# Attention with two steps' values products in even steps and small work in odd ones, and with statistics and the split of q and k behind their products

## The chip, the core and the metric

The kernel runs on one core of one Trainium2 chip. The core has a matrix engine (TensorE, PE in the profile, with its weight loads as PEld), a vector engine (VectorE, DVE), a scalar engine (ScalarE, ACT), GpSimd (POOL) and SyncE (SP), which mostly issues DMA transfers. Each engine runs its own instructions in order; between engines, semaphores hold an instruction back until its inputs and its output buffer are ready. Matrix products land in PSUM, eight banks of 128 partitions x 512 fp32 values.

The metric is the device time in microseconds (us) of one execution. The kernel before takes 2402.26 us, the median of 3 runs (2398.78 to 2404.74).

## The reference

One transformer layer on `x` of shape (2, 2048, 256) in fp32, cut here to what matters:

```
qkv  = x @ qkv_w + qkv_b                 # 16 heads of 16; q and k rotated per head
attn = softmax(q @ k.T / 4) @ v          # per head, over 2048 keys
x    = layernorm(x + attn @ out_w + out_b)
n    = layernorm(x, g1, be1)
x2   = x + n + (n @ mix_w + mix_b)
n2   = layernorm(x2, g2, be2)
w    = the two largest of softmax(n2 @ router_w), others 0      # 8 experts
moe  = sum over e of w[e] * (silu(n2 @ w1[e] + b1[e]) @ w2[e] + b2[e])
out  = layernorm(x + x2 + moe)
```

Every token goes through two of eight experts. The expert stage works on lists of tokens by expert, so it can start on a list only when the tokens of the blocks before are placed.

## The kernel before

**Attention.** The work is cut into 32 visits: 2 batches x 4 blocks of 512 queries x 4 groups of 4 heads. A visit has 16 steps, one for each 128 keys, so there are 512 steps. One step does four things:

- `scores` (L466), twice, one call for each pair of heads: two products of keys and queries (L470), two that add the negative row maximum (L479), each on 64 rows of the array so that two run side by side, into the four banks of `ps_sc`; then two exponentials on ScalarE (L485) into `ex`, eight buffers.
- `maxima` (L414), twice, called the first and the second half of a step here: two products (L426) into banks of `ps_mx`, and two reduces on VectorE (L434) that take the maximum of 512 scores for each of 128 queries. These maxima are needed 20 steps later (`AHEAD`), when `scores` of the next visit starts. The three banks of `ps_mx` are handed out in turn, to the maxima and to all small work alike (`bank`, L314).
- `values` (L492): four products of `ex` and the values, one for each head, each on 32 columns of the array (L500), added up over a visit's 16 steps in one bank, `ps_av`. A product of fp32 data counts as two matmul instructions in the trace, so one call shows as eight. After step 16, `attn_out` copies the sum to `avs` on ScalarE (L515), and one step later `divide` transposes it (`ps_o`) and divides by the sums of exponentials on VectorE (L525, L526).
- small work, described below.

The order on TensorE, ScalarE, VectorE and SyncE is the order of the program. For one step it is: `scores` twice, first half of the maxima, small work, `values` of the step before, second half.

**Small work.** A small planner holds two heaps, `todo`, one for urgent items and one for others. `later(steps, fn, cost, urgent)` (L290) puts a function in, due `steps` steps from now. `work(budget)` (L295) takes due items, urgent ones first and then by due time, and takes the cost of each off the budget until it is used up; an item may exceed it. Each step calls `work(1.0)`. A group of four transposes costs 0.5, a pair of products 2.0, VectorE work alone mostly 0. The items are:

- `prep_x`, `prep_qk`, `prep_v`: transposes of `x`, the products for q and k (`ps_qk`) and the values (`ps_v`). `prep_qk` also splits its result into a high and a low part: ScalarE copies it to `full` (L352), VectorE masks the high part (L354), GpSimd subtracts (L358) and issues four DMAs to a stack in DRAM (L362). `load_k` and `load_q` read the stacks back on SyncE's queue (L388), for the visit they serve.
- `rows_of` (L455, urgent): transposes of the maxima (`ps_m`).
- a chain for each block of 512 tokens once its four groups are done, from `block` (L585): transposes (`ps_oT`), `two_products` with the output weights (`ps_p`, L561), then `norms` (L616), transposes (`ps_nT`), `two_products` with the mixing weights (`ps_mix`), `lists` (L686), transposes (`ps_n2T`), router logits (`ps_l`), the choice of two experts (`choose`, L783), places in the lists (`ps_before`), and the experts' bias (`ps_c`, `ps_b`). `two_products` (L555) adds its product to the running sum on VectorE (L568) and then takes mean and variance of two rows of 128 tokens there (`bn_stats`, `bn_aggr`, L571 and L572). `norms` and `lists` follow one step after the second product.

There are eight blocks. The chain of the last one runs in the expert stage, where `between` (L1150) moves the planner's clock on by one and calls `work(1.0)`.

**Before attention**, the weights of q and k are rotated on VectorE (L266 to L268), with the cosines and sines in `cs` and temporaries `t1` and `t2`, and the first maxima run for 20 steps alone (the lead stage, `leading[0]` true), which use the banks of `ps_sc`.

**After attention**, 46 tiles of tokens go through the experts (`hidden` L1155, `add_tile` L1172), with their weights loaded on SyncE's queue (`load_tile` L1099). The first list is made by `early_tiles` (L973), five steps after the block before the last has placed its tokens.

Of the kernel before, what the change touches and what calls it, by code (L numbers as in the profile page):

```python
# [24 lines left out]
F32 = mybir.dt.float32  # L25
# [38 lines left out]
def seq_postln_kernel(  # L64
# [88 lines left out]
    with ExitStack() as actx:  # L153
# [38 lines left out]
        with tc.tile_pool(name="wraw", bufs=1) as wp:  # L192
            wr = bp.tile([P, 2, H, 3, HD], F32, name="wr", tag="zx", bufs=1)
            cs = wp.tile([P, 2, H, 8], F32, name="cs")
# [62 lines left out]
            for c in range(2):  # L257
                for s in range(2):
                    u1, u2 = wr[:, c, :, s, 0:8], wr[:, c, :, s, 8:16]
                    for dst, a, b_, op in (  # L260
                        (wqk[:, c, s, :, 0:8], u1, u2, ALU.subtract),
                        (wqk[:, c, s, :, 8:16], u2, u1, ALU.add),
                    ):
# [74 lines left out]
        def prep_qk(b, tb, s, hh):  # L338

            full, hi = (  # L340
                ep.tile([P, 512], F32, name=k, tag=k, bufs=2) for k in ("full", "hi")
            )
            ps = bank("ps_qk", 512)
            for c in range(2):
                nc.tensor.matmul(  # L345
                    ps,
                    lhsT=wqk[:, c, s, 8 * hh : 8 * hh + 8, :].rearrange("p h d -> p (h d)"),
                    rhs=xT[b, tb][:, c, :],
                    start=(c == 0),
                    stop=(c == 1),  # L350
                )
            nc.scalar.activation(full, ps, AF.Identity, bias=bqk[:, s, hh : hh + 1])  # L352

            nc.vector.tensor_single_scalar(  # L354
                hi.bitcast(I32), full.bitcast(I32), HIGH, ALU.bitwise_and
            )
            lo = full
            nc.gpsimd.tensor_sub(lo, full, hi)  # L358
# [4 lines left out]
            stack[b, tb, s, hh] = t  # L363

# [101 lines left out]
        def scores(w, kt, pair):  # L466
# [16 lines left out]
            for j in range(2):  # L483
                ex = ap_.tile([P, 512], F32, name="ex", tag="ex", bufs=8)
# [25 lines left out]
        def attn_out(w):  # L510
# [3 lines left out]
            avs = bp.tile([P, 512], F32, name="avs", tag="avs", bufs=2)  # L514
# [40 lines left out]
        def two_products(name, turned_in, w, k, sum_, mv):  # L555
# [29 lines left out]
        def block(b, qb):  # L585
# [30 lines left out]
        def norms(n, xr, mv, eng, pitch, gap):  # L616
# [447 lines left out]
        with tc.manual_schedule(engines={ET.PE, ET.Activation, ET.DVE, ET.SP}):  # L1064
# [6 lines left out]
            before = None  # L1071
            for t in range(NSTEP):
# [258 lines left out]
```

## Time and profile before

The profiled execution took 2406.82 us; its span, from first to last instruction, is 2405.1 us. All rows are of that execution.

| what | value |
|---|---|
| profiled execution, its span | 2406.82 us, 2405.1 us |
| lead stage ends, first step starts | 123.69 us |
| last step starts | 1793.27 us |
| last group of the expert stage's products (L1176) starts | 2360.48 us |
| VectorE reduces of the maxima (L434) | 2048 x 682 ns |
| ScalarE exponentials (L485) | 2048 x 603 ns |
| VectorE `bn_stats` (L571), `bn_aggr` (L572) | 64 x 411 ns, 64 x 182 ns |
| VectorE add of a product (L568) | 32 x 688 ns |
| VectorE mask (L354), GpSimd subtraction (L358) | 32 x 440 ns, 32 x 1279 ns |

A mean of one instruction includes its start and end latency, so instructions of one kind that follow each other start closer together than their duration. A matmul's end is modelled in the profile: it is safer to read the distance between the starts of successive groups than a duration. From first to last step 1670 us go by, 69% of the span; the granted clock of TensorE is 0.76 in the stretch 60 to 120 us, 0.90 in 120 to 180, and 1.00 in nearly all later stretches of attention.

### The profile page before, as it was taken

How to read it: one execution, taken by the hardware profiler on the slowest of the kernel's cores; microseconds unless marked ns; L12 is line 12 of the kernel's file. 1: busy time of each engine (PE TensorE's matmuls, PEld its weight loads, DVE VectorE, ACT ScalarE, POOL GpSimd, SP SyncE). 2: the span in 40 equal slices, each digit the busy share in tenths (PEclk: the TensorE clock that was granted, in tenths of full speed). 3: DMA queues.
4: the chain of work that ended last, by engine and by line, in shares of the span. 5: the costliest groups of instructions: out<-in, count | busy, mean ns of one | idle time of the engine just before them, and what ended most of it. 6: DMA issues, size and time to landing. Idle time of an engine off the chain costs nothing.

```text
span 2405.1 us, 39739 instructions
## 1 busy us (share of the span) xinstructions
PE 2277.9 (95%) x14270; PEld 1363.8 (57%) x14270; DVE 1534.9 (64%) x3060; ACT 1374.4 (57%) x2722; POOL 512.7 (21%) x863
## 2 busy tenths in 40 slices
PE   5899999999999999999999999999998899999993
PEld 2444555545545555555555555555547788888883
DVE  2678778868877887888888888888825111111113
ACT  1167667757766776777777667777773222223333
POOL 6212221140123022011211202202122322222113
PEclk7799999999999999999999999999999899999997
DMA  7516541141124211111311211221045466567994
GB/s 217 153 42 182 144 115 54 54 132 53 53 72 123 87 55 58 58 45 54 115 45 54 71 45 53 89 71 53 1 138 168 142 193 180 176 182 225 291 292 151
DMA packets 175516, 269.69 MB, mean 112 GB/s; under 512 B 29776, under 2 KB 109656, under 8 KB 175320
## 3 DMA queue, kind: packets, MB, share of 16 engines
q1 hardware_dynamic: 142648, 213.26, 25.9%
q0 software_dynamic: 32256, 52.98, 10.1%
q8 instruction: 113, 1.85, 0.3%
q10 hardware_dynamic: 416, 0.92, 0.1%
q14 instruction: 83, 0.68, 0.1%
HBM read 204.29 MB, written 62.74 MB: 111 GB/s over the span
## 4 chain that ended last, share of the span: by engine, by line
PE 77%; DVE 16%; DMA 3%; ACT 2%; issue 1%; POOL 1%; another core or an unknown queue 0%; SPq 0%; ACTq 0%; DVEq 0%; POOLq 0%
PE av L500 19%; PE ps_mx L426 13%; DVE pm L434 12%; PE ps_h L1161 11%; PE ps_y L1176 10%; PE ps_sc L470 6%; PE ps_sc L479 6%; PE ps_qk L345 2%; DMA st<-full 2%; PE ps_v L371 1%; PE ps_p L561 1%; PE ps_mix L561 1%; PE ps_m L458 1%; PE ps_o L522 1%; PE ps_b L766 1%
## 5 line engine op out<-in xcount | busy, mean ns | idle before, releaser
L434 DVE TENSOR_REDUCE pm<-ps_mx 128x1 f32<-128x512 f32 x2048 | 1273.2, 682 | 218.3 <-PE ps_mx L426 209.3
L485 ACT ACTIVATE ex<-ps_sc 128x512 f32<-128x512 f32 x2048 | 1058.1, 603 | 453.7 <-PE ps_sc L479 433.7
L426 PE MATMUL ps_mx<-km,qm 64*128 64x512 f32 x2048 | 580.5, 474 | 36.4 <-DMA km<-st 15.3
L426 PEld LDWEIGHTS ps_mx<-km,qm 64*128 64x128 f32 x2048 | 297.7, 186 | 556.2 <-DVE pm L434 357.4
L500 PE MATMUL av<-ex,vt 128*32 128x512 f32 x4096 | 547.3, 606 | 0.0
L470 PE MATMUL ps_sc<-qm,km 64*128 64x512 f32 x2048 | 435.4, 396 | 0.4 <-ACT ex L485 0.3
L479 PE MATMUL ps_sc<-mrow,sel 64*128 64x512 f32 x2048 | 428.6, 392 | 0.0
L1168 ACT ACTIVATE hT<-ps_h,b 128x256 f32<-128x256 f32 (+1 forms) x368 | 156.3, 425 | 378.3 <-PE ps_h L1161 361.9
L1161 PE MATMUL ps_h<-xT,w 128*128 128x256 f32 (+1 forms) x1472 | 282.6, 342 | 17.2 <-issue 11.0
L1161 PEld LDWEIGHTS ps_h<-xT,w 128*128 128x128 f32 x1472 | 231.6, 193 | 62.4 <-ACT hT L1168 21.7
L1176 PE MATMUL ps_y<-w,hT 128*128 128x256 f32 x1136 | 253.7, 379 | 0.0
L479 PEld LDWEIGHTS ps_sc<-mrow,sel 64*128 64x128 f32 x2048 | 216.7, 185 | 40.5
L470 PEld LDWEIGHTS ps_sc<-qm,km 64*128 64x128 f32 x2048 | 214.8, 186 | 42.0 <-ACT ex L485 18.3
L1176 PEld LDWEIGHTS ps_y<-w,hT 128*128 128x128 f32 x1136 | 212.1, 190 | 27.5 <-issue 0.7
L1140 DVE TENSOR_SCALAR xT<-ps_x,cols_sb 128x256 f32<-128x256 f32 (+1 forms) x92 | 40.2, 478 | 271.4 <-PE ps_x L1136 271.4
L1187 POOL DMA_INDIRECT acc<-y,xg x71 | 110.1, 1551 | 390.8 <-DVE y L1186 307.0
L500 PEld LDWEIGHTS av<-ex,vt 128*32 128x32 f32 x4096 | 80.9, 108 | 133.7 <-issue 132.6
L1186 DVE TENSOR_SCALAR y<-ps_y,xg 128x256 f32<-128x256 f32 x71 | 34.2, 483 | 187.8 <-PE ps_y L1176 187.6
L132 POOL TENSOR_SCALAR op_mul<-mv 128x4 f32<-128x4 f32 x18 | 4.2, 233 | 492.7 <-DVE mv L572 491.7
L358 POOL TENSOR_TENSOR full<-full,hi 128x512 f32<-128x512 f32 x32 | 40.9, 1279 | 239.5 <-DVE hi L354 239.4
L345 PE MATMUL ps_qk<-xT,wqk 128*128 128x512 f32 x128 | 73.3, 700 | 4.8 <-ACT xT L336 1.5
L857 POOL DMA_INDIRECT x_list<-zx,at_i x64 | 64.1, 1002 | 16.5 <-issue 13.6
(198 smaller groups left out, 1160.4 us busy)
## 6 DMA issues: line engine op xcount, KB each, us to landing
w<-in_w SPq DMA_DIRECT2D x92, 1024.0 KB
km<-st SPq DMA_DIRECT2D x256, 256.0 KB
st<-hi POOLq DMA_DIRECT2D x64, 256.0 KB
st<-full POOLq DMA_DIRECT2D x64, 256.0 KB
qm<-st SPq DMA_DIRECT2D x64, 256.0 KB
xg<-x_list SPq DMA_DIRECT2D x25, 258.0 KB
x_in<-in_x SPq DMA_DIRECT2D x8, 512.0 KB
xr<-in_x SPq DMA_DIRECT2D x8, 512.0 KB
```

The lines of the kernel that those rows point to most:

```text
L345: nc.tensor.matmul(ps, lhsT=wqk[:, c, s, 8 * hh : 8 * hh + 8, :].rearrange("p h d -> p (h d)"), rhs=xT[b, tb][:, c, :], start=(c == 0), st ...
L426: nc.tensor.matmul(ps[j], lhsT=qm[w][pair][r, qt * P : (qt + 1) * P], rhs=km[w][pair][r, kb * 512 : (kb + 1) * 512], start=True, stop=True,)
L434: nc.vector.tensor_reduce(pm[w][:, qt, 2 * pair + j, kb : kb + 1], ps[j], AX.X, ALU.max)
L470: nc.tensor.matmul(sc[j], lhsT=km[w][pair][r, kt * P : (kt + 1) * P], rhs=qm[w][pair][r, :], start=True, stop=False,)
L479: nc.tensor.matmul(sc[j], lhsT=sel[pair][r, :], rhs=mrow[w][r, :], start=False, stop=True)
L485: nc.scalar.activation(ex, sc[j], AF.Exp, scale=0.25)
L500: nc.tensor.matmul(av[32 * h : 32 * h + 32, :], lhsT=vt[b][:, kt, at : at + 32], rhs=exs[h], start=(kt == 0), stop=(kt == 15),)
L857: ins = nc.gpsimd.indirect_dma_start(out=x_list, out_offset=bass.IndirectOffsetOnAxis(ap=at_i[:, k, i : i + 1], axis=0), in_=zx[:, k, i, : ...
L1161: nc.tensor.matmul(ps, lhsT=w1t[:, c, k * P : (k + 1) * P], rhs=xT[:, c, :], start=(c == 0), stop=(c == 1),)
L1168: nc.scalar.activation(hT[:, k, :], ps, AF.Silu, bias=b1[:, k : k + 1])
L1176: nc.tensor.matmul(ps, lhsT=hT[:, k, s * P : (s + 1) * P], rhs=w2t[:, k, :], start=(k == 0), stop=(k == NFC - 1),)
L1187: nc.gpsimd.indirect_dma_start(out=acc, out_offset=bass.IndirectOffsetOnAxis(ap=xg[:, s, D : D + 1].bitcast(I32), axis=0), in_=y, in_offse ...
```

## The change

The main loop, the planner's `work` and four places in the small work change.

1. **Main loop.** Exponentials of a step go to a list, `waiting`. In an even step no small work with a cost runs; items of cost 0 that are due are run (`work(0)`), and then `values` for all waiting steps. In an odd step `work(1.0)` runs; if it spent less than 0.4, items of cost 0 and the waiting values follow as in an even step, else the values wait for the next step, which then has two of them. `ex` gets twelve buffers in place of eight.
2. **`work`** returns what it spent, and with a budget of 0 takes items of cost 0 alone.
3. **`prep_qk`**: after the lead stage, the mask, the subtraction and the four DMAs to the stack are an item of their own, one step later.
4. **`two_products`**: the statistics of its two rows of tokens become two items, one and two steps later; `norms` and `lists` come three steps after the second product in place of one.
5. **Buffers**: `avs` has one in place of two; `cs` and the temporaries of the rotation (now `rot`, with four pairs) share the memory of `x2` and `fT`, which the chain uses later.

```diff
-            cs = wp.tile([P, 2, H, 8], F32, name="cs")
+            cs = bp.tile([P, 2, H, 8], F32, name="cs", tag="x2", bufs=1)
+            rot = bp.tile([P, 4, 2, H, 8], F32, name="rot", tag="fT", bufs=1)
...
-                        t1 = wp.tile([P, H, 8], F32, name="t1", tag="t1", bufs=2)
-                        t2 = wp.tile([P, H, 8], F32, name="t2", tag="t2", bufs=2)
+                        t1, t2 = rot[:, 2 * (s % 2) + k, 0], rot[:, 2 * (s % 2) + k, 1]
...
         def work(budget):
+
+            spent = 0.0
             for heap in todo:
-                while heap and heap[0][0] <= now[0] and budget > 0:
-                    _, _, cost, fn = heappop(heap)
-                    fn()
-                    budget -= cost
+                kept = []
+                while heap and heap[0][0] <= now[0] and (spent < budget or budget == 0):
+                    item = heappop(heap)
+                    if budget == 0 and item[2] > 0:
+                        kept.append(item)
+                        continue
+                    item[3]()
+                    spent += item[2]
+                for item in kept:
+                    heappush(heap, item)
+            return spent
...
-            for r, part in enumerate((hi, lo, hi, lo) if s == 0 else (hi, hi, lo, lo)):
-                nc.gpsimd.dma_start(out=t[:, r], in_=part)
             stack[b, tb, s, hh] = t
+
+            def split():
+
+                nc.vector.tensor_single_scalar(
+                    hi.bitcast(I32), full.bitcast(I32), HIGH, ALU.bitwise_and
+                )
+                lo = full
+                nc.gpsimd.tensor_sub(lo, full, hi)
+                for r, part in enumerate((hi, lo, hi, lo) if s == 0 else (hi, hi, lo, lo)):
+                    nc.gpsimd.dma_start(out=t[:, r], in_=part)
+
+            if leading[0]:
+                split()
+            else:
+                later(1, split)
...
-                ex = ap_.tile([P, 512], F32, name="ex", tag="ex", bufs=8)
+                ex = ap_.tile([P, 512], F32, name="ex", tag="ex", bufs=12)
...
-            avs = bp.tile([P, 512], F32, name="avs", tag="avs", bufs=2)
+            avs = bp.tile([P, 512], F32, name="avs", tag="avs", bufs=1)
...
-            for i in range(2 * k, 2 * k + 2):
+
+            def moments(i):
                 st = bp.tile([P, 6], F32, name="st", tag="st", bufs=3)
                 nc.vector.bn_stats(st, sum_[:, i, :])
                 nc.vector.bn_aggr(mv[:, i, :], st)
+
+            for i in range(2):
+                later(1 + i, lambda i=i: moments(2 * k + i))
...
-                    later(1, lambda: norms(n, xr, mv, eng, pitch, gap))
+                    later(3, lambda: norms(n, xr, mv, eng, pitch, gap))
...
-                    later(1, lambda: lists(n, xr, x2, mv2, eng, gap))
+                    later(3, lambda: lists(n, xr, x2, mv2, eng, gap))
...
-            before = None
+
+            waiting: list = []
             for t in range(NSTEP):
                 now[0] = t
                 w, kt = divmod(t, 16)
                 exs = scores(w, kt, 0) + scores(w, kt, 1)
                 max_step(t + AHEAD, 0)
-                work(1.0)
-                if before is not None:
-                    values(*before)
+                if t % 2 == 0 or work(1.0) < 0.4:
+                    work(0)
+                    while waiting:
+                        values(*waiting.pop(0))
                 max_step(t + AHEAD, 1)
-                before = (w, kt, exs)
-            values(*before)
+                waiting.append((w, kt, exs))
+            while waiting:
+                values(*waiting.pop(0))
```

More of the change, by code (lines that the diff above doesn't have):

```diff
@@ L259, in seq_postln_kernel @@
                     u1, u2 = wr[:, c, :, s, 0:8], wr[:, c, :, s, 8:16]
-                    for dst, a, b_, op in (
-                        (wqk[:, c, s, :, 0:8], u1, u2, ALU.subtract),
-                        (wqk[:, c, s, :, 8:16], u2, u1, ALU.add),
-                    ):
-                        t1 = wp.tile([P, H, 8], F32, name="t1", tag="t1", bufs=2)
-                        t2 = wp.tile([P, H, 8], F32, name="t2", tag="t2", bufs=2)
+                    for k, (dst, a, b_, op) in enumerate(
+                        (
+                            (wqk[:, c, s, :, 0:8], u1, u2, ALU.subtract),
+                            (wqk[:, c, s, :, 8:16], u2, u1, ALU.add),
+                        )
+                    ):
+                        t1, t2 = rot[:, 2 * (s % 2) + k, 0], rot[:, 2 * (s % 2) + k, 1]
                         nc.vector.tensor_mul(t1, a, cs[:, 0])
@@ L352, in prep_qk @@
             nc.scalar.activation(full, ps, AF.Identity, bias=bqk[:, s, hh : hh + 1])
[L354 to L358, printed above, removed]
             name = f"st_{b}_{tb}_{s}_{hh}"
             t = dp.tile([8, 4, HD, 512], F32, name=name, tag=name)
-            for r, part in enumerate((hi, lo, hi, lo) if s == 0 else (hi, hi, lo, lo)):
-                nc.gpsimd.dma_start(out=t[:, r], in_=part)
             stack[b, tb, s, hh] = t
+            def split():
+                nc.vector.tensor_single_scalar(
+                    hi.bitcast(I32), full.bitcast(I32), HIGH, ALU.bitwise_and
+                )
+                lo = full
[6 more added lines that the diff above has]
+                later(1, split)
         def prep_v(b, kt):
```

## The prediction

> **What bounds the kernel now.** I read the busy shares first, then busy time by stretch, then the timeline of a few steps. The page's shares say TensorE:
>
> ```profile
> PE 2277.9 (95%) x14270; PEld 1363.8 (57%) x14270; DVE 1534.9 (64%) x3060; ACT 1374.4 (57%) x2722; POOL 512.7 (21%) x863
> PE 77%; DVE 16%; DMA 3%; ACT 2%; issue 1%; POOL 1%; another core or an unknown queue 0%; SPq 0%; ACTq 0%; DVEq 0%; POOLq 0%
> ```
>
> The second line is the chain that ended last: VectorE is 16% of it, nearly all L434. The stretch 1020 to 1080 us (columns: length, then busy us of each engine, granted clock, DMA) shows why it isn't idle behind TensorE:
>
> ```profile
> 1020.00:1080.00 60.00, 58.80 (x412) 30.74 (x404) 51.77 (x96) 43.08 (x85) 10.47 (x20) 1.00 0.13 45
> ```
>
> VectorE is busy 86% where the whole page says 64%. The timeline of one plain step (start, duration, engine, line) shows how the two interlock:
>
> ```profile
> 1042.37 0.52 PE L426 MATMUL ps_mx<-km,qm 64*128 64x512 f32 x2
> ...
> 1042.81 1.06 PE L500 MATMUL av<-ex,vt 128*32 128x512 f32 x8
> ...
> 1043.81 0.50 PE L426 MATMUL ps_mx<-km,qm 64*128 64x512 f32 x2
> ...
> 1044.15 0.39 PE L470 MATMUL ps_sc<-qm,km 64*128 64x512 f32 x2
> ...
> 1044.35 2.48 DVE L434 TENSOR_REDUCE pm<-ps_mx 128x1 f32<-128x512 f32 x4 [0.22 <-PE ps_mx L426]
> ```
>
> From first half to values 0.44 us, values to second half 1.00, to the scores 0.34, and the scores take 0.92 (next first half at 1045.07): 2.70. Four reduces take 2.48, so VectorE has 0.22 to spare. A reduce starts 0.53 after its product (1043.81 to 1044.35), the next follows 0.60 later, and one lasts 0.68. Of the 512 steps 309 are plain; transposes add 0.77 (3.46), `ps_o` 0.83 (3.52), a 512-wide product pair (`ps_p`, `ps_mix`, `ps_qk`, `ps_v`) 2.1 (4.80).
>
> **What a double values product costs.** The end of attention has two values products in a row:
>
> ```profile
> 1794.75 0.16 PEld L500 LDWEIGHTS av<-ex,vt 128*32 128x32 f32 x8 [0.36 <-issue]
> 1794.75 2.51 PE L500 MATMUL av<-ex,vt 128*32 128x512 f32 x16
> 1795.21 0.13 PEld L500 LDWEIGHTS av<-ex,vt 128*32 128x32 f32 x2 [0.30 <-ACT ex L485]
> ```
>
> The second one's first weights go in 0.46 after the start, while the first still streams (1.06); one pass is some 0.43, so a second product adds 2 x 0.43 = 0.85, not 1.00. Here a rule speaks against the change: the Trainium skill ("TensorE: Matmul & The Clock Gate", section "The mechanism") lets weights load beside a running matmul only when row groups differ, and these four column tiles share all rows. By it the second product costs 1.00 again; by the row 0.85. With 153 double products that is 23 us. I take the row. The same skill ("TensorEngine Tiling (Array Packing)", "Key Properties") says that a change of tiling mode drains the array. That drain is what a double product saves, and the rows price it at only 0.15 (1.00 less 0.85) on one side and about 0.10 on the other (0.33, where nothing is late, less the 0.23 between row-tiled pairs). If small work leaves the array as values do, which I assume since eight 256-wide products take 1.93 to `av` (L561) and also 1.93 to L426 in the lead stage (104.96 to 106.89), a merged pair saves 0.15: 153 x 0.15 = 23 us at best.
>
> **What it uncovers.** Only odd steps with small work drop their values; in the changed order 153 of 256 pairs do, the others keep one product per step. In such an odd step nothing long stands between first and second half. Both halves and the small work rotate through three banks of `ps_mx`: first half takes banks 1 and 2, small work 3, second half 1 and 2 again. So the second half waits for the reduces of the first. Before, the 1.00 of the values covered that. The trace has one step without values, the first:
>
> ```profile
> 126.37 1.05 PE L426 MATMUL ps_mx<-km,qm 64*128 64x512 f32 x3
> ...
> 127.06 2.48 DVE L434 TENSOR_REDUCE pm<-ps_mx 128x1 f32<-128x512 f32 x4 [1.64 <-PE ps_sc L479]
> 127.81 0.79 PE L426 MATMUL ps_mx<-km,qm 64*128 64x512 f32 x1 [0.39 <-DVE pm L434]
> ```
>
> There the fourth product waits for the first reduce: 127.06 + 0.68 is 127.74, released 0.07 later. With small work holding the third bank it would wait for the second reduce.
>
> Let T be the start of the first half in an odd step. Reduces run T+0.53 and T+1.13 to T+1.81; the last product of the second half starts at T+1.86. Transposes alone would have let it start at T+0.62+0.58+0.11 = T+1.31. After such a late product the scores run split; the row shows the price:
>
> ```profile
> 1002.12 0.18 PEld L426 LDWEIGHTS ps_mx<-km,qm 64*128 64x128 f32 x1 [0.17 <-ACT oT L548]
> ...
> 1003.16 0.61 PE L426 MATMUL ps_mx<-km,qm 64*128 64x512 f32 x2
> ...
> 1003.70 1.06 PE L500 MATMUL av<-ex,vt 128*32 128x512 f32 x8
> ```
>
> 1.57 from the late product to the values. A pair (T to the next T) is then 1.86 + 1.57 + 1.85 + 1.26 = 6.54 (1.85 = 1.00 + 0.85; 1.26 = 0.34 + 0.92). Before, a plain step and one with transposes were 2.69 + 3.46 = 6.15. **The pair loses 0.39.**
>
> By kind, in the same way:
> - Two transposes groups, which now fall into one odd step (2 x 0.5 of budget): the last product needs the first group's bank, and ScalarE empties it only after four exponentials, which end at T+1.86, plus 0.71 to 0.80. 7.3 to 7.4, before 2 x 3.46 = 6.92.
> - Product pairs: the second half is ready at T+0.62+1.93 = 2.55, past any reduce. The add (0.69) delays the reduces behind it, and the even step's first half waits 0.3. 7.55 against 4.80 + 2.70 = 7.50, without the statistics.
> - VectorE work d between the halves of an odd step makes the even step wait d - 0.63: `rd`, `otok` (0.67) nothing worth counting; with a pair of statistics (0.59) 0.63; with the second choice (1.4) 1.47.
> - In a plain step d costs the next one d - 0.21: statistics 0.38, first choice (five small ops, 1.05) 0.84.
>
> **Moved work.** The statistics, 0.59 per row block, leave the step of their product. Before, they made the following steps 3.10, 3.19, 4.34 (with `ps_m` and the norms behind it), 3.16 and 3.07 for 2.70, 2.70, 3.46, 2.70, 2.70: 2.6 us in 64 steps, which I credit wholly; the smaller waits where they land are debited above. The split of q and k (0.44 on VectorE, 1.28 on GpSimd, four GpSimd DMA issues of 0.6) comes one step later, about 3 us: loads of `km` and `qm` are due many steps behind, and TensorE waits for `km` once, 15.3 us in all, in the lead stage, where the split stays in place. SyncE only receives later dependencies. Cost nothing; if a load were late, one wait of up to 3 us. VectorE's wait for `full` (77.4 us in all) isn't on the path: the product after it is later still. The start's buffers (`cs`, `rot`) leave the 24 rotation ops of 0.28 as they are: -1 to +1, I take 0. Twelve `ex` buffers only permit the delay. One `avs` buffer: its transposes come a step after the copy and the next copy 15 later: 0.
>
> **The sum.** I take the 64 steps 256 to 319, one whole chain of small work; the trace has them in 1193.51 - 988.98 = 204.5 us. After: four pairs with `ps_o` 6.6, 6.6, 7.2, 8.0; three with double transposes 22.1; four product pairs 30.2; three with `ps_m` 19.8; `ps_m` with the logits 7.8; `ps_c` 6.5; two with `ps_b` 13.2; the step with `ps_before` 3.5; 27 plain steps 72.6 and their waits 2.0. Sum 206.2: 1.7 more. Seven chains lie in attention: +12. The remainder: eight `ps_o`/`ps_m` pairs before the first chain +3; some 27 pairs with `ps_qk` or `ps_v`, -0.2 each, -6; four double `x` transposes +2. The expert stage keeps its 1.73 per eight products. Its first lists come five steps (12 us) later: loads issued at 1771.7 had about 26 us to the stage's start, a first weight of 1 MB at that stretch's 178 GB/s needs 6, so 0 to +5: +2. Total +13. The profiled execution took 2406.8 (span 2405.1), so it would be about 2420; from the median of the runs, 2402.3, **2415**.
>
> **Rivals.** 0.3%, 7 us, is what a measurement of this kernel can tell from no change.
> - Forecast, slower by 3 to 26 us: 53%, of which 5 lie under 7 us.
> - **The bank wait hardly forms (faster).** Place: second half of the odd step. Without any bank waits the 64 steps would take some 10.5 us less (0.64 for each short pair, 0.85 for each double transpose, and the 2.2 of waits behind `ps_o`). If half is hidden, -5.2 + 1.7 = -3.5, times 7, is -25 and with the remainder 2376. It decides once the last product starts before about T+1.77, since 13 us over 153 pairs is 0.09 each. For it: double products leave VectorE idle in even steps. Against: three banks do not let it work ahead into odd ones. 20%.
> - The second values product pays 1.00, by the rule: +23, so 2438. Against it is one instance with the row above, which ran without maxima. 15%.
> - Gains in the chain's statistics and losses of banks cancel, within 7 us: 12%.
>
> That little merges is no separate case: 153 is counted from the order. So faster 20%, same 17%, slower 63%. The range 2385 to 2440 leaves out half of the bank rival and the worst of the third.
>
> **What would show it.** After: 16-matmul groups of values with 1.85 to the next product; in odd steps L426 idle behind L434 some 0.5 us, and odd steps of 2.9 us where 2.5 would do; double transposes with L426 waiting for ScalarE. If odd steps last 2.5, the bank step is wrong and the time goes under 2395; if the double product takes 2.0, the third case holds. Steps after `ps_p` should be free of backlog; if 3.1 remains there, the credit of 2.6 is wrong.

## The result, and the profile after

The changed kernel takes **2415.75 us** (median of 7 runs, 2411.35 to 2420.32), the kernel before 2402.26 in the same series (7 runs, 2397.18 to 2410.99). The ratio is **1.0047, 95% interval 1.0031 to 1.0062**: slower by some 11 us by the ratio (13.5 between the medians). The forecast was 2415. In a later series both came out lower, 2398.07 and 2387.03, with the same ratio, 1.0047 (1.0033 to 1.0062). Its chip is called the second here; on which chip the first series ran is not on record. The level is not the chip's alone: in a third series, on the second chip, the kernel before took 2406.58 (one run).

The page of the changed kernel, first the busy shares, then the chain that ended last:

```profile
PE 2262.1 (94%) x14270; PEld 1373.1 (57%) x14270; DVE 1535.3 (64%) x3060; ACT 1376.2 (57%) x2722; POOL 512.3 (21%) x863
PE 78%; DVE 10%; ACT 5%; DMA 3%; issue 1%; POOL 1%; another core or an unknown queue 0%; SPq 0%; ACTq 0%; POOLq 0%; DVEq 0%
```

The busy times hardly move: the work is the same. TensorE's busy time fell by 15.8 us while the span grew by 4.5, so by the page the new time is TensorE waiting. In the chain VectorE fell from 16% to 10% (12% and 8% are the reduces of the maxima, L434 and L452) and ScalarE rose from 2% to 5%. The prediction had let ScalarE hold back TensorE only where two groups of transposes fall into one step.

Lines have moved: L444 is the product of the maxima (L426 before), L452 their reduce (L434), L488 and L497 the scores, L503 the exponentials (L485), L518 the values (L500), L476 and L478 the turning of the maxima and its copy to `mrow`.

A step is counted here from the first product of its scores to that of the next step. The distance from the first step's first product to the last step's, and what lies behind it, in three pairs of profiled executions (us; the expert column is from the first to the last turned tile):

| run | first step starts | 512 steps | expert stage | span |
|---|---|---|---|---|
| before | 123.7 | 1669.6 | 554.4 | 2405.1 |
| after | 120.2 | 1691.0 | 541.4 | 2409.6 |
| before, second chip | 122.5 | 1668.6 | 537.4 | 2384.7 |
| after, second chip | 121.8 | 1683.0 | 534.2 | 2396.4 |

Attention lost 21.4 and 14.4 us; 11 were forecast (12 for seven chains, less 1). The expert stage gave 3.2 us back on the second chip, where 2 were forecast as a loss. The 13.0 of the first pair are mostly not the change's: in both its profiles, in the stretch 1850 to 1900 us, ScalarE stood idle ahead of its activation of `hT` for a releaser that the profile only calls "remote" (10.4 us in two waits before, 14.1 in three after), and TensorE was busy 39.31 of 50 us at a granted clock of 0.83 before, 42.30 at 0.93 after. It fell on both kernels, and by 10 us unequally: the expert stages are 17.0 and 7.2 longer than on the second chip. The two kernels with short reduces (the last experiment) show it too, though they ran on the second chip:

```profile
ACT hT L1168 <- remote: 10.4, 2, 5.2
ACT hT L1168 <- remote: 10.6, 3, 5.8
```

The first line is of the kernel before, the second of the kernel before with short reduces (waited for: us in total, times, longest); their expert stages last 554.4 and 554.3. So the wait is not bound to a chip. The other ten profiles do not have it. The four that do are also those in which no time of landing of a DMA is recorded, so the releaser may be a DMA; that stays open.

Of the 511 steps that can be compared in the two profiles of the changed kernel, 487 repeat to 0.02 us, but 14 single ones differ by 0.4 to 1.6 and hold 7.8 of the 8.0 us between 1691.0 and 1683.0. So the reading below rests on steps, and on medians of runs for totals; an attention that differs by a few us in single profiles shows nothing by itself.

### The profile page after: what moved, and what is told of

Its sections match the earlier page's. It is cut to its first block, busy times and chain, and to the rows that moved or that the text cites. A ratio compares the mean times of both kernels' runs of the same rounds, so it can differ in the third digit from the quotient of the medians.

```text
span 2409.6 us, 39733 instructions
## 1 busy us (share of the span) xinstructions
PE 2262.1 (94%) x14270; PEld 1373.1 (57%) x14270; DVE 1535.3 (64%) x3060; ACT 1376.2 (57%) x2722; POOL 512.3 (21%) x863
## 3 DMA queue, kind: packets, MB, share of 16 engines
q8 instruction: 113, 1.85, 0.3%
## 4 chain that ended last, share of the span: by engine, by line
PE 78%; DVE 10%; ACT 5%; DMA 3%; issue 1%; POOL 1%; another core or an unknown queue 0%; SPq 0%; ACTq 0%; POOLq 0%; DVEq 0%
PE av L518 19%; PE ps_mx L444 15%; PE ps_h L1186 10%; PE ps_y L1201 10%; DVE pm L452 8%; PE ps_sc L488 8%; PE ps_sc L497 7%; ACT ex L503 3%; PE ps_qk L356 2%; DMA st<-full 2%; PE ps_v L389 1%; PE ps_p L579 1%; PE ps_mix L579 1%; PE ps_b L788 1%; PE ps_x L1161 1%
## 5 line engine op out<-in xcount | busy, mean ns | idle before, releaser
L452 DVE TENSOR_REDUCE pm<-ps_mx 128x1 f32<-128x512 f32 x2048 | 1278.2, 682 | 278.2 <-PE ps_mx L444 268.5
L503 ACT ACTIVATE ex<-ps_sc 128x512 f32<-128x512 f32 x2048 | 1057.9, 602 | 467.9 <-PE ps_sc L497 446.9
L444 PE MATMUL ps_mx<-km,qm 64*128 64x512 f32 x2048 | 600.9, 473 | 65.5 <-DMA km<-st 16.5
L444 PEld LDWEIGHTS ps_mx<-km,qm 64*128 64x128 f32 x2048 | 302.7, 186 | 517.8 <-DVE pm L452 318.5
L518 PE MATMUL av<-ex,vt 128*32 128x512 f32 x4096 | 516.3, 603 | 0.0
L488 PE MATMUL ps_sc<-qm,km 64*128 64x512 f32 x2048 | 449.0, 400 | 0.1
L497 PE MATMUL ps_sc<-mrow,sel 64*128 64x512 f32 x2048 | 439.4, 394 | 0.0
L1186 PE MATMUL ps_h<-xT,w 128*128 128x256 f32 (+1 forms) x1472 | 276.2, 337 | 11.1 <-ACT hT L1193 6.4
L497 PEld LDWEIGHTS ps_sc<-mrow,sel 64*128 64x128 f32 x2048 | 228.2, 186 | 41.8
L488 PEld LDWEIGHTS ps_sc<-qm,km 64*128 64x128 f32 x2048 | 223.0, 186 | 37.6 <-ACT ex L503 15.6
L518 PEld LDWEIGHTS av<-ex,vt 128*32 128x32 f32 x4096 | 96.8, 109 | 188.1 <-issue 186.3
```

Of the source, the lines that this page charges most:

```text
L444: nc.tensor.matmul(ps[j], lhsT=qm[w][pair][r, qt * P : (qt + 1) * P], rhs=km[w][pair][r, kb * 512 : (kb + 1) * 512], start=True, stop=True,)
L452: nc.vector.tensor_reduce(pm[w][:, qt, 2 * pair + j, kb : kb + 1], ps[j], AX.X, ALU.max)
L488: nc.tensor.matmul(sc[j], lhsT=km[w][pair][r, kt * P : (kt + 1) * P], rhs=qm[w][pair][r, :], start=True, stop=False,)
L497: nc.tensor.matmul(sc[j], lhsT=sel[pair][r, :], rhs=mrow[w][r, :], start=False, stop=True)
L503: nc.scalar.activation(ex, sc[j], AF.Exp, scale=0.25)
L518: nc.tensor.matmul(av[32 * h : 32 * h + 32, :], lhsT=vt[b][:, kt, at : at + 32], rhs=exs[h], start=(kt == 0), stop=(kt == 15),)
```

## What the steps show

**The double values product costs what the row of the prediction said.** Timeline of the changed kernel at the end of a double step (start, duration, engine, line):

```profile
997.86 1.92 PE L518 MATMUL av<-ex,vt 128*32 128x512 f32 x16
...
999.71 0.49 PE L444 MATMUL ps_mx<-km,qm 64*128 64x512 f32 x2
```

1.85 from the values to the next first half, so 0.85 for the second product. An even step whose odd neighbour uncovered nothing lasts 3.55, which is 2.70 + 0.85. And a pair with `ps_qk` takes 3.80 + 3.56 = 7.36, 0.14 under the 7.50 of before: that is the 0.15 of the merged pair.

**The bank wait on VectorE forms as forecast.** The same visit, an odd step with `ps_o`, whose first half starts at 994.41:

```profile
994.41 0.51 PE L444 MATMUL ps_mx<-km,qm 64*128 64x512 f32 x2
...
995.67 0.18 PEld L444 LDWEIGHTS ps_mx<-km,qm 64*128 64x128 f32 x1 [0.17 <-DVE pm L452]
...
996.21 0.18 PEld L444 LDWEIGHTS ps_mx<-km,qm 64*128 64x128 f32 x1 [0.36 <-DVE pm L452]
996.22 0.29 PEld L488 LDWEIGHTS ps_sc<-qm,km 64*128 64x128 f32 x2
```

Each weight load of the second half stands behind one reduce. The last is released 1.80 after the first half's start; forecast was T + 1.86. From first half to first half the odd step takes 2.83, where 2.9 was forecast (2.74 from scores to scores).

**In a step with `ps_m` another engine holds the bank.** An odd step whose first half starts at 1034.35:

```profile
1034.13 2.06 ACT L503 ACTIVATE ex<-ps_sc 128x512 f32<-128x512 f32 x4 [1.66 <-PE ps_sc L497]
1034.35 0.57 PE L444 MATMUL ps_mx<-km,qm 64*128 64x512 f32 x2
...
1035.61 0.49 PE L444 MATMUL ps_mx<-km,qm 64*128 64x512 f32 x1
1036.06 0.62 ACT L478 CAST mrow<-ps_m 128x512 fp32r<-128x512 f32 x1
...
1036.73 0.49 PE L444 MATMUL ps_mx<-km,qm 64*128 64x512 f32 x1 [0.62 <-ACT mrow L478]
```

`ps_m` was done at about 1035.7 (1035.02 + 0.66), but its copy is queued on ScalarE behind four exponentials and starts at 1036.06. The last product of the second half waits for that copy, not for a reduce, and starts 2.38 after T. The step takes 3.3 to 3.4. With two groups of transposes the same occurs, as forecast:

```profile
1002.69 1.29 ACT L566 ACTIVATE oT<-ps_oT,rows_sb 128x512 f32<-128x512 f32 x2
1003.45 0.50 PE L444 MATMUL ps_mx<-km,qm 64*128 64x512 f32 x2 [0.62 <-ACT oT L566]
```

Its first half starts at 1000.97, so the second half comes 2.48 later.

By kind, for the most frequent kinds, one pair being an odd step and the even one behind it (us; means on the second chip; the last column is the run long_only, told below):

| small work | pairs | forecast | after | long_only |
|---|---|---|---|---|
| `ps_o` | 22 | 6.6 to 8.0 | 6.92 | 6.34 |
| `ps_m` | 17 | 6.54 | 7.14 | 6.36 |
| `ps_c` | 4 | 6.54 | 7.02 | 6.23 |
| `ps_b` | 11 | 6.54 | 6.69 | 6.66 |
| two of `ps_oT`, `ps_nT` | 14 | 7.3 to 7.4 | 7.30, 7.27 | 6.75, 6.79 |
| `ps_p`, `ps_mix` | 26 | 7.55 | 7.54, 7.57 | 7.54, 7.57 |
| `ps_qk`, `ps_v` | 21 | 7.30 | 7.36, 7.36 | 7.36, 7.36 |

Where ScalarE empties one group (`ps_m`, `ps_c`) the forecast was 0.5 to 0.6 short; elsewhere it stood within 0.15.

## The experiments

The theory under test had three parts: values moved away from the odd step uncover bank waits of VectorE and ScalarE (a loss); the second values product costs 0.85; delayed statistics are a gain, as the prediction had credited them. The rivals gave the loss to one engine alone, or held that the statistics gain nothing by themselves.

### Statistics alone, values alone, and values only behind long work

Statistics alone: the kernel before with part 4 of the change.

```diff
-            for i in range(2 * k, 2 * k + 2):
+            def moments(i):
...
+            for i in range(2):
+                later(1 + i, lambda i=i: moments(2 * k + i))
...
-                    later(1, lambda: norms(n, xr, mv, eng, pitch, gap))
+                    later(3, lambda: norms(n, xr, mv, eng, pitch, gap))
...
-                    later(1, lambda: lists(n, xr, x2, mv2, eng, gap))
+                    later(3, lambda: lists(n, xr, x2, mv2, eng, gap))
```

> The kernel before with the delay of the statistics alone (two items one and two steps later, norms and lists three steps after their second product). Theory A: the delay frees VectorE's queue behind each product pair (2.6 us per chain of 64 steps, seven chains in attention: -18) and gives the last chain room in the expert stage (-13 in the trace of the changed kernel): 2402 - 31 = about 2371, within 2365 to 2385. Rival B: the statistics land in plain steps that have only 0.2 us of VectorE to spare, so attention gains under 5 us, and the expert stage's gain comes from the odd-step planning and not from the delay: 2395 to 2405.

Values alone: the changed kernel with the diff above reversed, and the split in place.

```diff
-            if leading[0]:
-                split()
-            else:
-                later(1, split)
+            split()
```

> The changed kernel with statistics, norms, lists and the split of q and k back at their product's step: only the double values products, the odd-step planning and the buffers remain. Theory A: attention loses the bank waits (+21 measured) and also the 18 us that the delay had given back, and the expert stage its -13: 2402 + 21 + 18 = about 2440, within 2430 to 2450. Rival B (the delay brings nothing): as the changed kernel or some us below, 2405 to 2418.

Values only behind long work: the changed kernel, in which transposes, `ps_o`, `ps_m` and the like keep the values beside them, and only a step that spent 1.9 or more drops them.

```diff
-                if t % 2 == 0 or work(1.0) < 0.4:
+                if t % 2 == 0 or work(1.0) < 1.9:
```

> The changed kernel with the limit for dropping the values raised from 0.4 to 1.9, so that only odd steps with a product pair drop them; transposes, logits and bias keep their values beside them. Theory A: short odd steps no longer uncover a wait for a bank of ps_mx, product pairs never had one (7.54 measured against 7.50 before); the delay's gains stay: 2415 - 21 - 18 = about 2376, within 2365 to 2388. Rival C (the loss lies in the halved number of steps open to small work, not in banks): stays at 2410 to 2420.

Measured on one chip, before at 2385.28:

| run | time | ratio (95%) | 512 steps | expert stage |
|---|---|---|---|---|
| stats_only | 2377.76 | 0.9969 (0.9958 to 0.9981) | 1666.1 | 534.6 |
| values_only | 2437.24 | 1.0223 (1.0206 to 1.0240) | 1719.5 | 537.4 |
| long_only | 2359.03 | **0.9893 (0.9875 to 0.9911)** | 1645.4 | 532.6 |

By the ratio theory A had 0.987, 1.016 and 0.989. It missed for the statistics (31 us expected, 7 found; rival B, at 2395 to 2405, stands at its edge), was right in direction and short in size for the values (52 us lost, 28 to 48 expected), and was met by long_only, where rival C falls.

Two parts of a change don't add up here. In the old order the statistics' delay brings attention nothing that can be told from the spread: 1666.1 against 1668.6, but 1665.4 in last_chain_only (below), which leaves attention as it was. The steps show why. The step behind the first `ps_p` of a chain and the two after it (steps 262 to 264) take 3.12 + 2.70 + 2.70 = 8.52 in before on the second chip, and 2.70 + 2.91 + 2.92 = 8.53 in stats_only. A plain step of stats_only in which a row block's statistics land (lines as in the kernel):

```profile
1005.55 0.41 DVE L572 BATCH_NORM_STATS2 st<-xr 128x6 f32<-128x256 f32 x1
...
1006.10 2.45 DVE L434 TENSOR_REDUCE pm<-ps_mx 128x1 f32<-128x512 f32 x4
...
1006.81 0.18 PEld L426 LDWEIGHTS ps_mx<-km,qm 64*128 64x128 f32 x1 [0.28 <-DVE pm L434]
```

An old plain step has 0.22 of VectorE to spare, so statistics that leave one step make the next product of maxima late in another. Moving the values without the two delays costs 51 us (1719.5 to 1668.6). So the delay of the statistics is worth nothing in the old order, and much in the new one (22.7 us, below).

long_only beats both kernels. Its 58 double steps lie only behind work that covers the reduces (3.80 in the odd step). Two groups of transposes keep the values between the halves, and ScalarE empties the first group's bank meanwhile:

```profile
981.15 0.50 PE L444 MATMUL ps_mx<-km,qm 64*128 64x512 f32 x2
...
982.87 1.29 ACT L566 ACTIVATE oT<-ps_oT,rows_sb 128x512 f32<-128x512 f32 x2
982.95 1.06 PE L518 MATMUL av<-ex,vt 128*32 128x512 f32 x8
...
983.94 0.50 PE L444 MATMUL ps_mx<-km,qm 64*128 64x512 f32 x2
```

The second half starts 0.99 after the values, without a wait. The pair takes 4.05 + 2.70 = 6.75 in place of 7.30 in the changed kernel and 2 x 3.46 = 6.92 before. Against the changed kernel the table above accounts for the gain: (6.92 - 6.34) x 22 + (7.14 - 6.36) x 17 + some 0.5 x 22 for the double transposes + 0.8 x 4 for `ps_c` is 40; the two attentions differ by 37.6. Against the kernel before, attention gained 23.2 us, of which the 0.14 of a merged pair, 58 times, is 8. How the rest is shared by the delays was not tested: long_only was not run without them.

### The last chain alone

The statistics of only the last block come later, in the kernel before. It is to tell what the expert stage has of it.

```diff
+                if len(ends) == NTB:
+                    later(1 + i, lambda i=i: moments(2 * k + i))
+                else:
+                    moments(2 * k + i)
...
-                    later(1, lambda: lists(n, xr, x2, mv2, eng, gap))
+                    later(3 if n == NTB - 1 else 1, lambda: lists(n, xr, x2, mv2, eng, gap))
```

> The kernel before with the delay of statistics, norms and lists for the last block alone, which runs beside the experts. Theory A: the expert stage's gain of 13 us is this delay, which lets TensorE meet the last chain's transposes after their inputs are ready: about 2389, attention unchanged (last step starts at 1793 again). Rival B: the gain came from other changes in that stretch; within 4 us of 2402.

It gave 2380.59, 0.9975 (0.9964 to 0.9985), with 1665.4 for attention and 532.6 for the expert stage: some 6 us less than before, between theory A (13) and rival B (at most 4).

The delay of the last chain does shorten the expert stage, by 3 to 5 us. The seven profiles that have it, without a remote wait and with the copy of `ps_c` on ScalarE (see below), take 532.6 to 534.6 us; the two without it, before on the second chip and values_only, both take 537.4. In these two TensorE stands idle for 3.9 us ahead of the second tile's products (L1161 in before), in the seven for 1.0.

The prediction's +2 us was for something else, the first lists, which this run leaves where they were. They are late in the changed kernel: there the first expert's weights are asked for 8.0 us before the last step starts, in before 19.6 (both on the second chip). Yet the first turned tile comes 4.66 us after that start in both. Late lists cost nothing.

### The pair again on a second chip, and the split's delay

The kernels before and after were run unchanged beside the next two, to hold profiles from one chip against each other.

> The kernel before, for a profile on the chip of this comparison. Attention should last 1669 us from first to last step again, as its steps repeat to 0.01 us; what differs from the first profile (554 us between the first and last turned tile of the experts) is the chip's or the execution's. If the changed kernel's gain of 13 us in the expert stage was real, this stage is longer here than in the changed kernel on the same chip by some 13 us; if it was the two executions', by under 6.

> The changed kernel, for a profile on the same chip: attention 1691 us again. Total against before: 1.0047 if the first comparison holds (+11 us); +16 to +20 if the expert stage's gain was only 5 us, as the delay of the last chain alone brought it.

The kernel before against itself gave 1.0003 (0.9994 to 1.0012), the changed one 1.0047 (1.0033 to 1.0062). The profiles are in the table of the first section. The expert stages differ by 3.2, so the 13 us of the first pair were mostly the two executions'. Attention came to 1683.0 for the 1691 expected, by the 14 single steps told there.

The split's delay: the changed kernel with `split()` in place, the statistics still delayed.

```diff
-            if leading[0]:
-                split()
-            else:
-                later(1, split)
+            split()
```

> The changed kernel with the mask, subtraction and DMAs of q and k back at their product's step. Theory D: without values in the step, VectorE's mask waits for ScalarE's copy of the product, which comes after four exponentials, and the second half's reduces wait behind the mask; the 64-step stretches 0 to 192 get back to 228, 225 and 225 us from 220, 219 and 220, so +18 us on the changed kernel, and stretches from 192 on stay as they are. Rival: these 18 us are the statistics' (inline in values_only too), then under +4.

2409.49, 1.0103 (1.0085 to 1.0121), attention 1696.8 against 1683.0: the delay is worth **13.8 us** (11.4 between the medians of the runs), where the prediction counted nothing. It lies in the first 192 steps, where `ps_qk` is: 21 even steps behind a `ps_qk` take 4.19 to 4.24 in place of 3.56, 14.0 us in all. Theory D had 18, as it laid the whole loss of these steps in values_only to the split; 5.9 of it is the statistics'. Its timeline in no_split_delay, lines counted as in that kernel:

```profile
316.22 0.50 PE L441 MATMUL ps_mx<-km,qm 64*128 64x512 f32 x2
...
316.38 0.69 ACT L363 ACTIVATE full<-ps_qk,bqk 128x512 f32<-128x512 f32 x1 [0.83 <-issue]
...
317.10 0.43 DVE L370 TENSOR_SCALAR hi<-full 128x512 int32<-128x512 int32 x1 [1.65 <-ACT full L363]
...
317.44 2.48 DVE L449 TENSOR_REDUCE pm<-ps_mx 128x1 f32<-128x512 f32 x4
...
318.18 0.50 PE L441 MATMUL ps_mx<-km,qm 64*128 64x512 f32 x1 [0.32 <-DVE pm L449]
318.61 1.92 PE L515 MATMUL av<-ex,vt 128*32 128x512 f32 x16
```

VectorE stands idle 1.65 us at the mask, because ScalarE writes `full` only at 316.38 to 317.07. ScalarE had been idle for 0.83 us before that, so the copy waits for the product, and not for exponentials as theory D had it. The reduces of the odd step's second half (its products start at 316.22) queue behind the mask, start at 317.44 in place of about 316.75, and the first half of the even step waits for their banks: its second product starts at 318.18. The wait for `full` was known in the kernel before, and set aside with "the product after it is later still". That held there. A step that drops its values brings the next product forward, and what was idle time at no cost becomes part of the path.

In this order the parts of the change in attention are: values moved +50.9, statistics delayed -22.7 (1719.5 to 1696.8), split delayed -13.8, together +14.4. They add up because each is the difference of two neighbours; in another order the shares would differ, as stats_only shows. values_only ran on another chip than the rest.

### The copies of ScalarE

Two copies that empty small work on ScalarE go to VectorE in the changed kernel.

```diff
-                nc.scalar.copy(t, ps)
+                nc.vector.tensor_copy(t, ps)
...
-                nc.scalar.copy(cT, ps)
+                nc.vector.tensor_copy(cT, ps)
```

> The changed kernel with the copies of ps_m and ps_c moved from ScalarE to VectorE. Theory E: in odd steps with ps_m or ps_c the last product of the second half waits for the bank of the small work, which ScalarE empties only after its four exponentials; on VectorE the copy follows the first half's reduces, so these odd steps fall from 3.3 to 3.4 to about 2.8, and some 25 pairs gain 0.3 to 0.5 each: 8 to 12 us less than the changed kernel. Rival (the wait is VectorE's own reduces): no gain, or a loss of some 0.1 a pair for 0.6 us more on VectorE.

Odd steps with `ps_m` fell from 3.38 to 2.89 and those with `ps_c` from 3.26 to 2.74, as a bank wait behind ScalarE would have it. Attention took 1677.5, 5.5 less, which is within what two executions of the changed kernel differ by. But the time was 2407.64, 1.0087 (1.0070 to 1.0104), 9.6 more than the changed kernel where theory E had 8 to 12 less: the expert stage took 548.8 in place of 534.2. The waits of TensorE from 1800 to 1920 us (waited for: us in total, times, longest), and the row of 1860 to 1880 (columns as in the prediction's such row):

```profile
PE ps_b L788 <- DVE cT L780: 10.0, 1, 10.0
```

```profile
1860.00:1880.00 20.00, 9.96 (x26) 6.48 (x25) 12.00 (x61) 1.23 (x3) 15.12 (x17) 0.66 0.28 100
```

TensorE idles half of these 20 us, at a granted clock of 0.66, because the last block's copy of `ps_c` stands on VectorE behind the making of lists. An engine that empties a bank sooner in attention empties another one later, 60 us after the last step.

### The copy of the maxima alone

To part the two effects, only the first of the two edits, in the changed kernel and in long_only:

> The changed kernel with the copy of ps_m to mrow alone on VectorE; the copy of ps_c stays on ScalarE. Theory (in odd steps with ps_m the last product of the second half waits for ScalarE's copy, behind four exponentials; what vector_copies lost in the expert stage came from the copy of ps_c in the last block): odd steps with ps_m near 2.9 us in place of 3.4, attention 1677 to 1681 us, experts 532 to 538, ratio to before 1.002 to 1.004. Rival (the 0.4 to 0.5 us come back one step later, as VectorE's reduces stand behind the copy): odd steps near 2.9 but attention 1683 +- 1, ratio 1.0047. Second rival (the loss in the expert stage came from any copy moved to VectorE): experts near 549, ratio near 1.009.

> The kernel in which only product pairs drop their values (long_only, ratio 0.9893), with the copy of ps_m to mrow on VectorE. Theory: steps with ps_m keep their values here, whose 1.00 us already covers the copy, so nothing is to be gained: ratio 0.988 to 0.991, steps with ps_m 3.6 to 3.7. Rival (ScalarE is late for the exponentials in these steps, so relieving it helps): ratio below 0.987.

maxima_copy_only: 2395.76, 1.0037 (1.0023 to 1.0050), attention 1682.2, expert stage 532.6. The expert stage's loss was the copy of `ps_c`, then. In attention the first rival is right in part: odd steps with `ps_m` take 2.89 in place of 3.38, but the even ones behind them 3.96 in place of 3.77, so 0.19 of the 0.49 comes back. The timeline of one such step:

```profile
1082.33 1.09 PE L444 MATMUL ps_mx<-km,qm 64*128 64x512 f32 x2
1082.78 0.68 DVE L478 CAST mrow<-ps_m 128x512 fp32r<-128x512 f32 x1
...
1083.38 2.48 DVE L452 TENSOR_REDUCE pm<-ps_mx 128x1 f32<-128x512 f32 x4
...
1084.12 0.18 PEld L444 LDWEIGHTS ps_mx<-km,qm 64*128 64x128 f32 x1 [0.20 <-DVE pm L452]
```

The second half no longer waits for ScalarE, but the reduces stand behind the copy, and the next step's products wait for them. A pair is 6.85 in place of 7.14; over 17 pairs 5 us, of which the whole attention shows 0.8: pairs with `ps_o` (+0.08 each) and a few single slow steps have the rest. The interval overlaps that of the changed kernel, so the total is unresolved. The wait behind ScalarE is shown; that the other engine could save it in the total is not.

long_maxima_copy: 2359.55, 0.9881 (0.9866 to 0.9896), attention 1647.7 against long_only's 1645.4. There values still lie between `ps_m` and the second half, and steps with `ps_m` take 3.65 in both. Nothing was to be gained, and nothing was.

### Reduces of a quarter of the length

In the kernels before and after the reduce of the maxima reads 128 of 512 keys, so three quarters of the keys are left out of the maxima. This makes VectorE fast and leaves TensorE's and ScalarE's work as it is.

```diff
-                    pm[w][:, qt, 2 * pair + j, kb : kb + 1], ps[j], AX.X, ALU.max
+                    pm[w][:, qt, 2 * pair + j, kb : kb + 1], ps[j][:, 0:128], AX.X, ALU.max
```

> The kernel before with each reduce of the maxima over 128 of its 512 scores, so that VectorE's part of a step falls from 2.5 to some 1.2 us; the maxima then cover a quarter of the keys. Both theories: plain steps lose the 0.1 us in which the last product of the first half waits for a reduce, 2.70 to 2.59, and the steps with waits behind VectorE's small work (3.1 to 3.5) fall to that too; attention about 1669 - 0.11 x 490 - 40 = 1575.

> The changed kernel with the same narrow reduces. Theory A: odd steps with ps_o, which waited for a reduce, fall from 2.74 to about 2.5; odd steps with ps_m, ps_c and two transposes wait for ScalarE's copy after four exponentials and stay within 0.1 of 3.4, 3.26, 3.5 to 3.75; so the changed kernel still takes more in attention than the kernel before with the same reduces, by 5 to 25 us. Rival F (reduces alone cause the loss): all short odd steps fall to about 2.5, and attention lies 20 us or more below that of the kernel before with the same reduces.

One run each gave 2251.41 and 2270.83, with attention at 1528.8 and 1562.9. If VectorE's banks were all that the changed order loses to, it should have come level or ahead with short reduces. It is 34 us behind in attention, more than with long ones and than the 5 to 25 expected. Both expectations were missed in size: attention of before fell by 140 us where 94 were expected, as steps with small work fell by more (3.46 to 3.17) than plain ones (2.70 to 2.58). And in narrow after the odd step with `ps_m` fell to 2.17 like that with `ps_o`, where the wait for ScalarE's copy was expected to keep it at 3.4. That wait had moved, into the even step:

```profile
959.58 0.62 ACT L478 CAST mrow<-ps_m 128x512 fp32r<-128x512 f32 x1
...
959.77 0.18 PEld L488 LDWEIGHTS ps_sc<-qm,km 64*128 64x128 f32 x1 [0.23 <-ACT ex L503]
...
960.25 0.19 PEld L444 LDWEIGHTS ps_mx<-km,qm 64*128 64x128 f32 x2 [0.19 <-ACT mrow L478]
```

The scores now wait for a bank that an exponential empties, and the first half for `mrow`. The pair takes 2.17 + 3.74 = 5.91 against 2.58 + 3.17 = 5.75 in narrow before. An odd step of 2.17 leaves ScalarE hardly more than the 2.07 of its four exponentials, and a copy of 0.62 on top does not fit. More than half of the 34 us comes from the 22 pairs with two groups of transposes. There the wait stayed in the odd step (3.32 to 3.50, where about 3.5 to 3.75 was expected), TensorE waits 15.1 us in all behind ScalarE's copies (`oT`, `nT`, `n2T`, `xT`), and the pairs take 7.1 to 7.3 against 2 x 3.17 = 6.34. With VectorE out of the way, ScalarE is what short odd steps run into.

## Why the prediction came true, and where it did not

The main mechanism was right: the odd step that drops its values waits for banks, and loses more than a double product saves. That the total came out right to 1 us is luck, as the sum held errors of both signs: attention lost 3 to 10 us more than forecast, and the expert stage gained where a loss was forecast.

- **Double product 0.85, merged pair -0.15**: right. The rule of the Trainium skill that was weighed ("TensorE: Matmul & The Clock Gate", section "The mechanism") would have made it 1.00 as the prediction read it; 1.85 from values to the next product decides for the row, and the rival of 2438 falls. The same section also lets weights go ahead when they are for a background weight buffer, so it does not force the 1.00; no trace here shows that buffer.
- **Bank wait of short odd steps**: right for `ps_o` (6.57 without other VectorE work, forecast 6.6; the fourth of a chain, with the second choice, 7.9, forecast 8.0). The rival that it hardly forms falls too.
- **`ps_m` and `ps_c` at 6.54**: wrong, by 0.5 to 0.6 a pair. What failed is to take these pairs to wait for a reduce, like `ps_o`. The three-bank argument was applied with ScalarE only where two groups of transposes fell together. It had to be asked of each small work who empties it, and what stands before that on the same engine. In steps 256 to 319 this is +1.6 for three `ps_m` pairs and +0.5 for `ps_c`, and the pair of `ps_m` with the logits took 8.14 (9.46 in the first profile) against 7.8. These 64 steps took 210.6 and 209.3 for a forecast of 206.2; the rest on the second chip is some 1.0 for step 256, an even step with two products of a pair begun one step earlier (3.73), which the sum had as a plain one. VectorE's moved work costs the plain steps it lands in 0.2 to 0.7 (2.92, 3.05, 3.12, 3.39), together 1.7 where 2.0 were forecast.
- **Credit of 2.6 per chain for statistics**: the backlog does go (3.12 to 2.70 behind a `ps_p`, the sign that the prediction had named), but that did not make it a gain. In the old order as much comes back where the statistics land. In the new one, where double steps (3.55 with 2.48 of reduces) leave VectorE idle for about 1.1, the delay is worth 22.7 us, 3.2 a chain after all landings. The sum had 2.6 less landing waits of up to 2.0.
- **Split of q and k at nothing**: the pair with `ps_qk` came out as forecast (7.36 for 7.30), but the reason given was wrong. With the split left in its place the new order would have lost 13.8 us more: the cover named for its wait, a later product, goes with the values.
- **Expert stage +2**: wrong in sign. Late lists cost nothing, and the delay of the last chain, which the prediction did not price, gains 3 to 5 us.
- **Seven equal chains**: wrong in distribution. By 64 steps the second chip's difference is -1.9, -0.6, +0.3 in the first 192 steps, where `ps_qk` and `ps_v` gain, and +4.8, +3.6, +3.6, +4.5 in the next 256, where transposes and maxima lose; the last 64 are level.

Why the scores' exponentials delay the even steps in narrow after was seen in one profile only, and the 0.29 by which its small steps in narrow before fell was not taken apart.

## What to carry to other kernels

Long work between two halves of a step is also cover: before it is moved, ask of each buffer that rotates there which engine empties it and what is queued before that on this engine. Batching pays where the step that gives up the work has another piece as long (1.9 us here), not where it keeps 0.6 us of transposes: the same mechanism used for 58 steps in place of 153 turned +0.5% into -1.1%. And a delay of side work is worth nothing where every step is full, but much once some steps have slack, so parts of a change have to be measured in the order in which they will run.

## What was not expected of the hardware

- A wait moved rather than vanished each time one engine was relieved: VectorE's reduce (0.36 us), ScalarE's copy (0.62 us), ScalarE's exponential (0.23 us) took turns in holding TensorE back in these steps.
- One copy of 0.67 us on the wrong queue stopped TensorE for 10.0 us, and the clock granted in that 20 us stretch was 0.66 against 0.91 in the same stretch of the changed kernel.
- Steps of one kind repeat to 0.01 or 0.02 us on different chips, while 14 single steps moved attention of the changed kernel by 8 us between two executions, and the expert stage of the kernel before took 554.4 and 537.4 us, with the "remote" waits in the first. The chip does not tell them apart: on one chip the kernel before took 2387.03 and, in another series, 2406.58.
